# Counting edges in groups of 125 with 12 targets: one-hots on three engines and count products pinned inside the units of a GNN and mixture-of-experts kernel

## The chip, the core and the metric

The kernel runs on one core of one Trainium2 chip. Its time is the device time in microseconds (us) of one execution; three executions were timed. A further execution was profiled, and all rows below come from that one.

## The reference, cut to what matters

1250 tokens of 1024 features go through a two-layer graph network over 40000 edges and then through a mixture of eight experts. Only the graph part is touched.

```python
def _sage_layer(h, edge_src, edge_dst, deg_inv, W_self, W_neigh, b):
    msg = h[edge_src]
    agg = jax.ops.segment_sum(msg, edge_dst, num_segments=h.shape[0])
    mean = agg * deg_inv[:, None]
    return h @ W_self + mean @ W_neigh + b
deg = jax.ops.segment_sum(jnp.ones_like(edge_dst, dtype=x.dtype), edge_dst, num_segments=N)
deg_inv = 1.0 / jnp.maximum(deg, 1.0)
h = jax.nn.relu(_sage_layer(x, edge_src, edge_dst, deg_inv, W_self0, W_neigh0, b0))
out = _sage_layer(h, edge_src, edge_dst, deg_inv, W_self1, W_neigh1, b1)
```

The edges come sorted by target (`edge_dst`).

## The kernel before

**Counts in place of a gather.** The segment sum is made a matrix product: a matrix C counts how often source s sends to target t, kept as 10 blocks of 128 sources by 1250 targets. The neighbour sum of a layer is then a product of C with the features, and the column sums of C are the degrees. C must be complete before the first of these products, at line 553.

**How C is filled.** The sorted edges are cut into 160 groups of 250 (`EG`), each two chunks of 125 edges (`GC`, `GP`). All targets of a group lie within 24 (`WIN`) of its first. For a chunk, GpSimd writes a one-hot `ol` of the source's lane (125 edges by 128 lanes, line 413), VectorE a one-hot `oh` of the source's block and the target's place in the window (125 by 10 x 24 = 240, line 420), and TensorE multiplies them (line 423). The two chunks of a group add up in PSUM tile `cnt`; VectorE then adds the 128 x 240 counts into C at the group's base (line 442). The base is a number in `base_i`, which VectorE's sequencer loads into a register (line 437) before the add can be issued. `row_of_groups` does two groups, four chunks, at a time; there are 80 rows. The adds of a row are issued two rows later (`open_rows`). If a group did not fit its window, `verdict` would say so and a second, general path would run after the first.

**What stands around it.** `self_unit` computes a 128-column piece of h @ W_self for a range of tokens: eight matrix products over k, each of 256, 498 or 496 columns. There are 24 of them. `y_unit` computes h @ W_neigh for 128 tokens, ten in the first quarter (q == 0); its result is split into a high part by ScalarE and a low part by VectorE (`split`, line 394). The whole of the counting is spread over self units and the ten y units of q == 0. After them come the column sums (line 553) and the products with C (line 564).

**What sets the order.** The opening, up to the first `turn_ranges`, is in an order written out by hand for VectorE, ScalarE and TensorE (`manual_schedule`). Rows of groups are then asked for by `some_groups(n)` ahead of a unit, and the scheduler of the build places each instruction in its engine's queue; each engine then runs its queue strictly in that order. `keep_in_program_order` pins an instruction against earlier pinned ones. `routing_constants` (small VectorE work, and a transfer of `eb2` that VectorE reads) is pinned so, after the units of q == 1.

**Buffers.** `hot` has six buffers for each of `ol` and `oh`; `pc` has three PSUM banks for `cnt`, so a row of groups can start only when the adds of the row three before it are done.

Of the kernel before, what the change touches and what calls it, by code (L numbers as in the profile page):

```python
# [20 lines left out]

P = 128
EPS = 1e-5
WIN = 24
GC, GP = 2, 125
LQ = 32


# [1 line left out]
def kernel(  # L30
# [28 lines left out]
    QW = D // 4  # L59
    NB = -(-N // P)  # L60
    NP = NB * P
    EG = GC * GP
    NGR = NE // EG
    R = NGR // 2
    WEXP = KD * H + KH * D
    NTILE = (2 * N) // P + E
    assert R * 2 * EG == NE and R <= P and 2 * NB * WIN <= 512 and N > WIN
    rows = [min(P, N - b * P) for b in range(NB)]

    step = -(-(N - 2 * P) // 4) * 2  # L70
# [72 lines left out]
    stt = nc.vector.scalar_tensor_tensor  # L143


    RE = 2 * EG
    assert 8 * RE <= 4000 and 3 * NGR <= 500 and 8480 + 6 * NGR <= 9440
    edge = L[:R, 4000:8000].rearrange("p (a n) -> p a n", n=RE)
    dst_i, src_i, hi_i, lo_i = (edge[:, a, :].bitcast(I32) for a in range(4))
    dst_f, hi_f, lo_f, key = (edge[:, a, :] for a in range(4, 8))  # L150
# [13 lines left out]
    nc.vector.memset(eps, EPS)  # L164

    nc.scalar.activation(small.tile([P, 1], F32, name="rs"), eps, AF.Sqrt)
    ident = const.tile([P, P], F32, name="ident")
    make_identity(nc, ident)

# [27 lines left out]
    nc.scalar.dma_start(out=b0_p, in_=b0.rearrange("(k p) -> p k", p=P))  # L197


    ext = const.tile([R, 3, 2], F32, name="ext")  # L200
    base_i = const.tile([1, NGR], I32, name="base_i")

    keys = const.tile([GP, 2, 2 * GC, R], F32, name="keys")
    worst = const.tile([1, 1], F32, name="worst")
    plain = const.tile([1, 1], I32, name="plain")
    gx = L[:1, 8000 : 8000 + 3 * NGR].rearrange("o (a g) -> o a g", a=3)
    lo_, hi_ = gx[:, 0, :], gx[:, 1, :]
    APART = 16
    assert APART * EG < 4096

    dst_halves = dst_f.rearrange("p (a n) -> p a n", a=2)

    def make_keys():

        nc.vector.tensor_reduce(ext[:, 0, :], dst_halves, AX.X, ALU.min)
        nc.vector.tensor_scalar(ext[:, 2, :], ext[:, 0, :], float(N - WIN), None, op0=ALU.min)
        nc.vector.tensor_scalar(hi_i, src_i, 7, None, op0=ALU.arith_shift_right)
        nc.vector.tensor_scalar(lo_i, src_i, P - 1, None, op0=ALU.bitwise_and)
        nc.vector.tensor_copy(hi_f, hi_i)
        nc.vector.tensor_copy(lo_f, lo_i)  # L220
        stt(key, hi_f, float(WIN), dst_f, op0=ALU.mult, op1=ALU.add)
        for i in range(2):
            part = key[:, i * EG : (i + 1) * EG]
            nc.vector.tensor_scalar(part, part, ext[:, 2, i : i + 1], None, op0=ALU.subtract)

    def turn_keys():
        for a, v in enumerate((key, lo_f)):
            ps = tpp.tile([P, 4, P], F32, name="tp")
            pf = ps.rearrange("p a b -> p (a b)")
            for c in range(2 * GC):  # L230
                nc.tensor.transpose(
                    pf[:GP, c * R : (c + 1) * R], v[:, c * GP : (c + 1) * GP], ident[:R, :R]
                )
            nc.scalar.copy(keys[:, a].rearrange("p c g -> p (c g)"), pf[:GP, : 2 * GC * R])

    def turn_ranges():

        nc.vector.tensor_reduce(ext[:, 1, :], dst_halves, AX.X, ALU.max)
        for a in (2, 0, 1):
            pe = tpp.tile([P, 4, P], F32, name="tp")  # L240
            for i in range(2):
                nc.tensor.transpose(pe[:1, i, :R], ext[:, a, i : i + 1], ident[:R, :R])
            nc.vector.tensor_copy(
                gx[:, a, :].rearrange("o (r i) -> o i r", i=2), pe[:1, :2, :R]
            )
            if a == 2:
                nc.vector.tensor_copy(base_i, gx[:, 2, :])

    def verdict():

        bad = L[:1, 8480 : 8480 + 6 * NGR].rearrange("o (a g) -> o a g", a=6)
        nc.vector.memset(bad, -1.0)
        stt(bad[:, 0, :], hi_, float(1 - WIN), lo_, op0=ALU.add, op1=ALU.subtract)
        nc.vector.tensor_tensor(bad[:, 1, : NGR - 1], lo_[:, : NGR - 1], lo_[:, 1:], ALU.subtract)
        nc.vector.tensor_tensor(bad[:, 2, : NGR - 1], hi_[:, : NGR - 1], hi_[:, 1:], ALU.subtract)
        stt(
            bad[:, 3, : NGR - APART], hi_[:, : NGR - APART], 1.0, lo_[:, APART:],
            op0=ALU.add, op1=ALU.subtract,
        )
        nc.vector.tensor_scalar(bad[:, 4, :], hi_, float(1 - N), None, op0=ALU.add)  # L260
        nc.vector.tensor_scalar(bad[:, 5, :], lo_, -1.0, None, op0=ALU.mult)
        nc.vector.tensor_reduce(worst, bad.rearrange("o a g -> o (a g)"), AX.X, ALU.max)
        nc.vector.tensor_scalar(plain, worst, 0.0, None, op0=ALU.is_le)
# [93 lines left out]
    def gnn_windows():  # L357
# [22 lines left out]

        y0 = ExitStack()
        yp = y0.enter_context(tc.tile_pool(name="yp", bufs=1, side="right"))
        hot = y0.enter_context(tc.tile_pool(name="hot", bufs=6, side="right"))

        yh = yp.tile([P, NB, QW], F32R, name="yh")
        yl = yp.tile([P, NB, QW], F32R, name="yl")
        win = yp.tile([P, NB * WIN], F16, name="win")
        win_i = yp.tile([P, NB * WIN], I32, name="win_i")
        nc.gpsimd.iota(win_i, pattern=[[1, NB * WIN]], base=0, channel_multiplier=0)
# [18 lines left out]
        GW = NB * WIN  # L408

        def row_of_groups(r):  # L410
            ol = hot.tile([GP, 2 * GC, P], F16, name="ol")
            for c in range(2 * GC):
                nc.gpsimd.tensor_scalar(  # L413
                    ol[:, c, :], lane[:GP], keys[:, 1, c, r : r + 1], None, op0=ALU.is_equal
                )
            ps = pc.tile([P, 2, 256], F32, name="cnt")
            for i in range(2):
                for c in range(GC):
                    oh = hot.tile([GP, GW], F16, name="oh")
                    nc.vector.tensor_scalar(  # L420
                        oh, win[:GP], keys[:, 0, i * GC + c, r : r + 1], None, op0=ALU.is_equal
                    )
                    nc.tensor.matmul(  # L423
                        ps[:, i, :GW], ol[:, i * GC + c, :], oh,
                        start=(c == 0), stop=(c == GC - 1),
                    )
            open_rows.append((r, ps))
            if len(open_rows) > 2:
                close_row()

        open_rows = []

        def close_row():
            r, ps = open_rows.pop(0)
            for i in range(2):
                g = 2 * r + i
                at = nc.values_load(
                    base_i[0:1, g : g + 1], engines=(ENG.DVE,), min_val=0, max_val=N - WIN,
                    skip_runtime_bounds_check_because="cut at N - WIN, and a target is never below 0",
                )  # L440
                to = C[:, :, ds(at, WIN)]
                nc.vector.tensor_tensor(  # L442
                    to, to.bitcast(F32),
                    ps[:, i, :GW].rearrange("p (k w) -> p k w", k=NB), ALU.add,
                )

        groups = iter(range(R))

# [4 lines left out]
                    row_of_groups(g)  # L453


        def self_unit(w, d, c, halfway=None):
            c0, n = cchunks[c]
            ps = mm.tile([P, 512], F32, name="ps")
            for k in range(KD):
                if halfway is not None and k == KD // 2:  # L460
                    halfway()
                nc.tensor.matmul(  # L462
                    ps[:, :n], w[:, k, (d % 2) * P : (d % 2 + 1) * P], h0T[:, k, c0 : c0 + n],
                    start=(k == 0), stop=(k == KD - 1),
                )
            nc.scalar.activation(
                hT1[:, d, c0 : c0 + n], ps[:, :n], AF.Identity, bias=b0_p[:, d : d + 1]
            )


        with tc.manual_schedule(engines={ENG.DVE, ENG.Activation, ENG.PE}):
            norm = [layernorm_steps(first_row_of(b), first_row_of(b), P) for b in range(6)]

            def step(*bs):
                for b in bs:
                    next(norm[b])

            step(0, 0, 1, 0, 1)
            turn_tokens(0)
            nc.vector.tensor_copy(dst_f, dst_i)  # L480
# [17 lines left out]
            clear(9)  # L498
            turn_ranges()
        w_next = load_q(w_self0, 1)  # L500
        some_groups(3)
        tokens(6)
        tokens(7)
        some_groups(2)
        self_unit(ws_first, 1, 1)
        tokens(8)
        tokens(9)
        some_groups(2)
        self_unit(ws_first, 0, 2)
        some_groups(2)  # L510
        self_unit(ws_first, 1, 2)
        verdict()
        for q in range(1, 4):
            w_q = w_next
            w_next = load_q(w_self0, q + 1) if q < 3 else load_q(w_neigh0, 0)
            for d in (2 * q, 2 * q + 1):
                for c in range(3):
                    some_groups(4 if c else 2)
                    self_unit(w_q, d, c)
            if q == 1:  # L520
                routing_constants()

# [13 lines left out]
        for q in range(4):  # L536
            w_q = w_next
            w_next = load_q(w_neigh0, q + 1) if q < 3 else None
            for b in range(NB):
                if q == 0:  # L540
                    some_groups(1)
                y_unit(w_q, h0T, b, yh[: rows[b], b, :], yl[: rows[b], b, :])
            if q == 3:
                w_half = load_half(w_neigh1, 0)
            if q == 0:
                some_groups(R)
                while open_rows:
                    close_row()

                for c0, n in cchunks:  # L550
                    ps = mm.tile([P, 512], F32, name="ps")
# [1130 lines left out]
```

## Time and profile before

| | us |
|---|---|
| runs shown: median (lowest to highest) | 1147.37 (1146.6 to 1149.48) |
| the profiled execution, its own time | 1146.48 |
| its span, first to last instruction | 1144.3 |
| first one-hot `oh` starts | 31.6 |
| first count product starts | 35.1 |
| last count product starts | 232.8 |
| column sums of C (line 553) start | 234.6 |
| busy from 28.6 to 234.6: TensorE, VectorE, ScalarE, GpSimd | 201.7, 153.9, 25.3, 193.2 |

The span is cut into 40 slices of 28.6 us. The counting lies in slices 2 to 9. A busy time counts an instruction from its start to its modelled end, so that a queue of short instructions can look fuller than it is; where a pace matters, the distance from one start to the next is the better number. A matrix product in 32-bit floats stands in the trace as two records.

### The profile page before, as it was taken

What the parts mean: (1) busy time and instruction counts of PE and PEld (TensorE: products, weight loads), DVE (VectorE), ACT (ScalarE), POOL (GpSimd) and SP (SyncE); (2) the same over time, 40 slices, a digit from 0 to 9 for tenths busy, and PEclk for the clock granted to TensorE, in tenths of its full rate; (3) what the DMA queues carried; (4) which work ended last, traced back from release to release, by engine and by line L of the source; (5) the groups of instructions that cost most, each with busy time, mean ns of one, the idle gap of its engine ahead of it and who ended that gap; (6) DMA issues with size and microseconds to landing.
All of it is one profiled execution on the core that took longest, in us unless ns stands there. A gap on an engine that the chain in (4) does not pass through costs nothing.

```text
span 1144.3 us, 13214 instructions
## 1 busy us (share of the span) xinstructions
PE 1108.3 (97%) x4775; PEld 791.2 (69%) x4775; DVE 451.1 (39%) x1129; ACT 181.5 (16%) x420; POOL 331.7 (29%) x438
## 2 busy tenths in 40 slices
PE   6999999999999999999999999999999989999994
PEld 4556556888888886887688778885444766666662
DVE  8777777761212154341224132555322542111110
ACT  5301000001111111100110000123011223222220
POOL 1899999800000000032003002342000013223221
PEclk9999999999999999999999999999999999999997
DMA  6110111010100021042004261335921435444542
GB/s 230 34 38 5 38 38 38 1 37 1 38 1 1 1 74 38 1 154 93 7 10 168 88 222 42 117 148 209 373 60 37 150 92 136 112 113 105 127 115 45
DMA packets 59330, 95.40 MB, mean 83 GB/s; under 512 B 8797, under 2 KB 35645, under 8 KB 59251
## 3 DMA queue, kind: packets, MB, share of 16 engines
q1 hardware_dynamic: 48400, 67.72, 17.3%
q0 software_dynamic: 7056, 23.88, 9.2%
q10 hardware_dynamic: 3798, 2.84, 0.8%
q8 instruction: 42, 0.69, 0.2%
q14 instruction: 34, 0.28, 0.1%
HBM read 68.76 MB, written 27.47 MB: 84 GB/s over the span
## 4 chain that ended last, share of the span: by engine, by line
PE 93%; DVE 2%; ACT 1%; DMA 1%; POOL 1%; issue 0%; ACTq 0%; DVEq 0%; POOLq 0%
PE ps L528 12%; PE ps L462 11%; PE psb L642 9%; PE ps L712 8%; PE ps L564 8%; PE ps L642 7%; PE ps L1516 7%; PE ps L1541 7%; PE ps L1188 5%; PE ps L629 5%; PE ps L1202 4%; PE cnt L423 3%; PE tp L1504 2%; PE ps L1141 2%; PE ps L1537 1%; PE tp L322 1%
## 5 line engine op out<-in xcount | busy, mean ns | idle before, releaser
L413 POOL TENSOR_SCALAR ol<-lane,keys 125x128 f16<-125x128 f16 x320 | 193.2, 622 | 27.6 <-DVE oh L420 27.6
L462 PE MATMUL ps<-h0T,L 128*128 128x498 f32 (+2 forms) x384 | 147.4, 518 | 0.2 <-ACT h0T L325 0.2
L528 PE MATMUL ps<-L,h0T 128*128 128x256 f32 (+1 forms) x640 | 142.0, 380 | 0.0
L708 POOL TENSOR_TENSOR L<-L 128x512 f32<-128x512 f32 (+1 forms) x20 | 31.4, 1576 | 375.1 <-DMA L<-in_L_gnn_b_dram 216.5
L528 PEld LDWEIGHTS ps<-L,h0T 128*128 128x128 f32 (+1 forms) x640 | 118.7, 188 | 17.7 <-issue 0.5
L420 DVE TENSOR_SCALAR oh<-win,keys 125x240 f16<-125x240 f16 x320 | 84.7, 322 | 32.7 <-PE cnt L423 31.1
L462 PEld LDWEIGHTS ps<-h0T,L 128*128 128x128 f32 x384 | 68.1, 192 | 38.3 <-issue 33.9
L1516 PE MATMUL ps<-xw,L 128*128 x368 | 84.9, 384 | 0.4 <-issue 0.4
L1541 PE MATMUL ps<-xw,L 128*128 x184 | 83.5, 597 | 0.1
L564 PE MATMUL ps<-C,yh 128*128 128x256 f32 (+2 forms) x240 | 81.9, 356 | 0.0
L564 PE MATMUL ps<-C,yl 128*128 128x256 f32 (+2 forms) x240 | 81.5, 354 | 0.0
L712 PE MATMUL ps<-zh,C 128*128 128x512 f32 (+1 forms) x200 | 79.6, 398 | 0.0
L712 PE MATMUL ps<-zl,C 128*128 128x512 f32 (+1 forms) x200 | 78.7, 393 | 0.0
L1516 PEld LDWEIGHTS ps<-xw,L 128*128 128x128 f32 x368 | 69.2, 193 | 10.3 <-issue 1.8
L1552 POOL DMA_INDIRECT out_dram<-L x23 | 36.3, 1579 | 133.5 <-ACT L L1505 87.9
L442 DVE TENSOR_TENSOR C<-C,cnt 128x240 f32 x160 | 64.3, 402 | 12.5 <-DVE oh L420 1.6
L1493 POOL DMA_INDIRECT L<-t_d,L x26 | 26.0, 1000 | 148.1 <-DVE L L141 127.8
L1541 PEld LDWEIGHTS ps<-xw,L 128*128 128x128 f32 x184 | 33.3, 190 | 35.3 <-issue 32.9
L423 PEld LDWEIGHTS <-ol 125*128 125x128 f16 x320 | 30.9, 97 | 36.7 <-POOL ol L413 20.0
L1549 DVE TENSOR_SCALAR L<-ps,L 128x512 f32<-128x512 f32 x23 | 17.3, 751 | 91.8 <-PE ps L1541 91.8
L394 DVE TENSOR_TENSOR yl<-ps,yh 128x256 fp32r<-128x256 f32 (+1 forms) x40 | 16.9, 424 | 92.1 <-ACT yh L393 92.1
L423 PE MATMUL cnt<-oh,ol 125*128 125x240 f16 x320 | 50.0, 266 | 2.6 <-POOL ol L413 2.1
(226 smaller groups left out, 1504.3 us busy)
## 6 DMA issues: line engine op xcount, KB each, us to landing
xw<-in_L_ffn_ew_dram SPq DMA_DIRECT2D x16, 1024.0 KB, 7.6
L<-in_x_dram SPq DMA_DIRECT2D x20, 256.0 KB, 2.8
v_d<-L SPq DMA_DIRECT2D x18, 256.0 KB, 2.0
xa<-v_d SPq DMA_DIRECT2D x18, 256.0 KB, 6.0
t_d<-L SPq DMA_DIRECT2D x9, 512.0 KB, 4.0
out_dram<-xa SPq DMA_DIRECT2D x9, 512.0 KB, 3.7
L<-in_L_gnn_W_self_dram SPq DMA_DIRECT2D x4, 1024.0 KB, 5.4
L<-in_L_gnn_W_neigh_dram SPq DMA_DIRECT2D x4, 1024.0 KB
```

Source lines behind the costliest of these rows:

```text
L413: nc.gpsimd.tensor_scalar(ol[:, c, :], lane[:GP], keys[:, 1, c, r : r + 1], None, op0=ALU.is_equal)
L420: nc.vector.tensor_scalar(oh, win[:GP], keys[:, 0, i * GC + c, r : r + 1], None, op0=ALU.is_equal)
L423: nc.tensor.matmul(ps[:, i, :GW], ol[:, i * GC + c, :], oh, start=(c == 0), stop=(c == GC - 1),)
L442: nc.vector.tensor_tensor(to, to.bitcast(F32), ps[:, i, :GW].rearrange("p (k w) -> p k w", k=NB), ALU.add,)
L462: nc.tensor.matmul(ps[:, :n], w[:, k, (d % 2) * P : (d % 2 + 1) * P], h0T[:, k, c0 : c0 + n], start=(k == 0), stop=(k == KD - 1),)
L528: nc.tensor.matmul(ps[:m, :QW], hT[:, k, blk(b)], w[:, k, :], start=(k == 0), stop=(k == KD - 1))
L564: nc.tensor.matmul(ps[:, :n], part[: rows[k], k, (d % 2) * P : (d % 2 + 1) * P], C[: rows[k], k, c0 : c0 + n], start=(k == 0 and part is y ...
L629: nc.tensor.matmul(ps[:m], hT1[:, k, blk(b)], w[:, k, :], start=(k == 0), stop=(k == KD - 1))
L642: nc.tensor.matmul(ps, rows_of(k), w[:, k, :], start=(first and k == 0), stop=(k == KB - 1), skip_group_check=not first,)
L712: nc.tensor.matmul(ps[:m], C[: rows[k], k, blk(b)], part[: rows[k], k, :], start=(k == 0 and part is yh), stop=(k == NB - 1 and part is yl),)
L1516: nc.tensor.matmul(ps[:, :H], xT[:, k, :], w1_all[:, ds(e, 1), k * H : (k + 1) * H], start=(k == 0), stop=(k == KD - 1),)
L1541: nc.tensor.matmul(ps, hT[:, q, :], w2_all[:, ds(e, 1), q * D + h * HALF : q * D + (h + 1) * HALF], start=False, stop=(q == KH - 1),)
```

## The change

- **Smaller groups.** A group is now one chunk of 125 edges with a window of 12 targets: `EG` = 125, `WIN` = 12, and `RG` = 4 groups in a row. There are still 80 rows and 320 count products, each of 120 columns in place of 240. Each product is a group of its own, so there are 320 adds of 128 x 120 in place of 160 of 128 x 240, each with its own register load.
- **One-hots spread.** Of a row's four `ol`, GpSimd makes two and ScalarE two, each by two activations, relu(1 - |key - lane|). Of its four `oh`, VectorE makes three and GpSimd the fourth.
- **Rings.** `oh` has 14 buffers, `ol` and the new `away` four.
- **Order.** VectorE's one-hots, the adds, the count products and the products of `self_unit` are pinned. `self_unit` takes a number of rows and spreads them over its eight products; the three units of a 128-column piece get 2, 4 and 3 rows. One add follows each product, eight groups behind. `y_unit` is not pinned. The last eight adds come after the last y unit in the program.
- **Opening.** Sixteen products of the identity with itself stand ahead of the first transposes.
- **Smaller things.** `base_i` has 320 numbers, and the rows of `verdict` are twice as long; `ext`, `base_i` and `keys` move to another pool; `bad` lies over the edge lists.

```diff
-WIN = 24
-GC, GP = 2, 125
+WIN = 12
+EG = 125
+RG = 4
...
-        hot = y0.enter_context(tc.tile_pool(name="hot", bufs=6, side="right"))
+        hot = y0.enter_context(tc.tile_pool(name="hot", bufs=4, side="right"))
+        hot_t = y0.enter_context(tc.tile_pool(name="hot_t", bufs=14, side="right"))
...
         def row_of_groups(r):
-            ol = hot.tile([GP, 2 * GC, P], F16, name="ol")
-            for c in range(2 * GC):
-                nc.gpsimd.tensor_scalar(
-                    ol[:, c, :], lane[:GP], keys[:, 1, c, r : r + 1], None, op0=ALU.is_equal
-                )
-            ps = pc.tile([P, 2, 256], F32, name="cnt")
-            for i in range(2):
-                for c in range(GC):
-                    oh = hot.tile([GP, GW], F16, name="oh")
-                    nc.vector.tensor_scalar(
-                        oh, win[:GP], keys[:, 0, i * GC + c, r : r + 1], None, op0=ALU.is_equal
-                    )
-                    nc.tensor.matmul(
-                        ps[:, i, :GW], ol[:, i * GC + c, :], oh,
-                        start=(c == 0), stop=(c == GC - 1),
-                    )
-            open_rows.append((r, ps))
-            if len(open_rows) > 2:
-                close_row()
...
+            ol = hot.tile([EG, RG, P], F16, name="ol")
+            for i in range(RG):
+                k = keys[:, 1, i, r : r + 1]
+                if i < 2:
+                    nc.gpsimd.tensor_scalar(ol[:, i, :], lane[:EG], k, None, op0=ALU.is_equal)
+                else:
+
+                    away = hot.tile([EG, P], F16, name="away")
+                    nc.scalar.activation(away, lane[:EG], AF.Abs, scale=-1.0, bias=k)
+                    nc.scalar.activation(ol[:, i, :], away, AF.Relu, scale=-1.0, bias=one_p[:EG])
+            ps = pc.tile([P, RG, P], F32, name="cnt")
+            for i in range(RG):
+                oh = hot_t.tile([EG, GW], F16, name="oh")
+                eng = nc.vector if i < RG - 1 else nc.gpsimd
+                made = eng.tensor_scalar(
+                    oh, win[:EG], keys[:, 0, i, r : r + 1], None, op0=ALU.is_equal
+                )
+                if i < RG - 1:
+                    pin(made)
+                pin(nc.tensor.matmul(ps[:, i, :GW], ol[:, i, :], oh, start=True, stop=True))
+
+                if len(to_add) >= 2 * RG:
+                    add_group()
+            to_add.extend((r, ps, i) for i in range(RG))
+
+        to_add = []
+        pin = tc.keep_in_program_order
+
+        def add_group():
+            r, ps, i = to_add.pop(0)
+            g = RG * r + i
+            at = nc.values_load(
+                base_i[0:1, g : g + 1], engines=(ENG.DVE,), min_val=0, max_val=N - WIN,
...
+            )
+            to = C[:, :, ds(at, WIN)]
+            tc.keep_in_program_order(
                 nc.vector.tensor_tensor(
                     to, to.bitcast(F32),
                     ps[:, i, :GW].rearrange("p (k w) -> p k w", k=NB), ALU.add,
                 )
+            )
...
-        def self_unit(w, d, c, halfway=None):
+        def self_unit(w, d, c, halfway=None, n_groups=0):
...
-                nc.tensor.matmul(
-                    ps[:, :n], w[:, k, (d % 2) * P : (d % 2 + 1) * P], h0T[:, k, c0 : c0 + n],
-                    start=(k == 0), stop=(k == KD - 1),
+                some_groups(((k + 1) * n_groups) // KD - (k * n_groups) // KD)
+                pin(
+                    nc.tensor.matmul(
+                        ps[:, :n], w[:, k, (d % 2) * P : (d % 2 + 1) * P], h0T[:, k, c0 : c0 + n],
+                        start=(k == 0), stop=(k == KD - 1),
+                    )
                 )
...
+            idle = mm.tile([P, 512], F32, name="ps")
+            for _ in range(16):
+                nc.tensor.matmul(idle[:, :P], ident, ident, start=True, stop=True)
             step(0, 0, 1, 0, 1)
...
         w_next = load_q(w_self0, 1)
-        some_groups(3)
-        tokens(6)
-        tokens(7)
-        some_groups(2)
-        self_unit(ws_first, 1, 1)
-        tokens(8)
-        tokens(9)
-        some_groups(2)
-        self_unit(ws_first, 0, 2)
-        some_groups(2)
-        self_unit(ws_first, 1, 2)
+        self_unit(ws_first, 1, 1, None, 3)
+        for b in range(6, NB):
+            tokens(b)
+            some_groups(1)
+        self_unit(ws_first, 0, 2, None, 3)
+        self_unit(ws_first, 1, 2, None, 3)
         verdict()
...
                 for c in range(3):
-                    some_groups(4 if c else 2)
-                    self_unit(w_q, d, c)
+                    self_unit(w_q, d, c, None, (2, 4, 3)[c])
...
                 if q == 0:
-                    some_groups(1)
+                    some_groups(2 if b < 4 else b < NB - 1)
                 y_unit(w_q, h0T, b, yh[: rows[b], b, :], yl[: rows[b], b, :])
...
                 some_groups(R)
-                while open_rows:
-                    close_row()
+                while to_add:
+                    add_group()
```

## The prediction

> **What bounds the kernel now.** I read the busy row and the slices first, then the chain of waits, then the groups, and last the records of single lines.
>
> ```profile
> PE 1108.3 (97%) x4775; PEld 791.2 (69%) x4775; DVE 451.1 (39%) x1129; ACT 181.5 (16%) x420; POOL 331.7 (29%) x438
> ...
> PE   6999999999999999999999999999999989999994
> PEld 4556556888888886887688778885444766666662
> DVE  8777777761212154341224132555322542111110
> ACT  5301000001111111100110000123011223222220
> POOL 1899999800000000032003002342000013223221
> ```
>
> TensorE (PE) is full from slice 2 on. But its weight loads (PEld) are thin in slices 2 to 8, and exactly there GpSimd (POOL) is full: the counting stage. All other stages are left as they are, so the change is worth what it does to the start of the column sums of C at 234.62 us; what follows is TensorE work in an unbroken chain, and moves with it.
>
> ```profile
> 229.16 3.47 PE ps L528 x16
> 234.62 6.00 PE ps L553 x30
> ```
>
> In the list of the chain the start comes first, then the length: the last-but-one y unit, and the column sums.
>
> ```profile
> L413 POOL TENSOR_SCALAR ol<-lane,keys 125x128 f16<-125x128 f16 x320 | 193.2, 622 | 27.6 <-DVE oh L420 27.6
> L420 DVE TENSOR_SCALAR oh<-win,keys 125x240 f16<-125x240 f16 x320 | 84.7, 322 | 32.7 <-PE cnt L423 31.1
> L442 DVE TENSOR_TENSOR C<-C,cnt 128x240 f32 x160 | 64.3, 402 | 12.5 <-DVE oh L420 1.6
> L423 PE MATMUL cnt<-oh,ol 125*128 125x240 f16 x320 | 50.0, 266 | 2.6 <-POOL ol L413 2.1
> ```
>
> GpSimd's 193.2 us run from 32.1 to 225 without a gap: 2.42 us a row of groups. Yet TensorE lost little by it: from one product's start to the next is 102 ns at the median, and over the 229 neighbouring pairs the excess is 28.5 - 229 x 0.102 = 5.1 us. Of the 198 us from the first product to the last, the products are 320 x 0.102 = 32.6.
>
> The number that decides is in the records of VectorE's sequencer (DVEq), which count as idle in the busy rows:
>
> ```profile
> L437 DVEq TENSOR_LOAD <-base_i x160: 297/303/551, 37.6 to 233.7; - x160
> ...
> L442 DVEq FUSED_REGOPS x160: 69/69/69, 38.3 to 234.0; - x160
> ```
>
> (least/median/most ns.) Each add needs a register load of 303 ns, a gap of 76, and register arithmetic of 69 before it is issued, and the next load starts only after that. From load to load with only an add between, 73 pairs in the trace have a median of 531 ns (least 513), although the add itself keeps the engine about 0.4 us. Today that is 160 x 0.53 = 85 us of 200, and hidden.
>
> **The change, part by part.**
>
> *Narrower products.* 120 columns in place of 240. The 240-column pitch of 102 ns is 2.4 columns a ns, so 120 columns are 51 ns, if the weight load keeps up. The Trainium skill, "TensorE: Matmul & The Clock Gate", section "Back-to-back issue gap", speaks against that: it gives a load-and-multiply pair about 81 ns at 128 columns. The rows that are near: at line 1359 pairs with 16-bit weights of 128x128 follow one another every 25 ns with 23 columns and 34 ns with 69. So the load isn't the floor here and I take 51: 320 x 0.051 = 16.3 us saved; by the page's figure 6.7.
>
> *GpSimd.* Two `ol` of 604 ns (193.2/320) and one `oh` of at most that: 1.8 us a row. TensorE asks for a row every 2.07 us in the units: a piece has 3.46 + 6.67 + 6.64 us of own products (pitches of 216 and 416 ns a record) and nine rows of 4 x 0.051 = 0.2. So GpSimd is no bound any more, and the 5.1 us of stalls go. ScalarE gets four activations a row; from its 128x256 cast (372 ns) and 128x1 activation (about 300) a 128-column one is about 0.33, so 1.3 a row beside 0.68 for every third: it fits, and the order waits of its queue cost nothing while rings are four rows deep.
>
> *What is late next: VectorE's sequencer.* Adds double to 320. Per row: four times 0.531 for load and add, three one-hots between loads at 0.035 (pairs with one one-hot between have 562 ns at least), and, as compiled, one add in four waits on two semaphores, which puts an extra event of 21 ns ahead (two such adds in the trace were 68 ns later). Sum 2.12 + 0.10 + 0.07 = **2.30 us a row**, against 2.07 that TensorE would take. The data path isn't the limit: 120 columns of add and one-hot are shorter than that. The Trainium skill, "DMA: Bandwidth & Descriptors", section "Latency and other measured facts", puts a register load's floor at about 600 ns; with 0.3 more per load a row would be 3.5 us, and 80 rows end 90 us later. The trace has 303 for this very load, so that is out.
>
> Now the pinned order: a product needs its one-hot, and the one-hots stand between the adds. TensorE can therefore not run ahead of VectorE by more than the one-hots allow, and waits.
>
> - 54 rows lie in the 18 units of q 1 to 3: 54 x (2.30 - 2.07) = 12.4 us.
> - `verdict` took 55.02 to 57.6 = 2.6 us of VectorE; rows twice as long add 0.17 (160 elements at 0.96 a ns, the slope between the 960-element reduction of 1.14 us and the 160-element ones) to four operations, 0.1 to two, 1.0 to the reduction: 4.5, of which a load behind it hides 0.5. It had slack before; now 4.0 are seen.
> - `routing_constants`: 1.6 us of small operations and 1.2 of casts; and the first cast waits for the `eb2` transfer, which landed 3.95 us after the last memset that SP's queue waits for. As compiled five adds (2.7) stand between, so 1.3 is waited for. Together 4.1; 4.5 with the row's late one-hots.
> - The third group of `turn_ranges` now waits for a copy with no product to fill in: 0.5.
>
> *The tail.* As compiled, the low-part split of the tenth y unit stands ahead of the last **eleven** adds in VectorE's queue. Today two adds stand there, and the column sums start 1.86 us after the last product:
>
> ```profile
> 233.05 0.42 DVE L394 TENSOR_TENSOR yl<-ps,yh 98x256 fp32r<-98x256 f32 x1 [1.32 <-ACT yh L393]
> 233.64 0.93 DVE L442 TENSOR_TENSOR C<-C,cnt 128x240 f32 x2 [0.16 <-DVE yl L394]
> ```
>
> After: the unit's drain 0.17 (its products are 380 ns long and 216 apart), ScalarE's half 0.37 (its cast at line 393), issue 0.1, 11 x 0.531 + 3 x 0.07 = 6.05, the last add 0.3: 7.0 us from the last y product.
>
> *Warm-up.* The identity is ready at 1.45 us, 16 products at the slow pitch of 213 ns end at 4.9, and the first transpose waits for VectorE until 9.10. TensorE's first 16 transposes ran at 213 ns each, later ones at 109; the speed changed near 15.2 (the granted clock in the windows says 1.00 throughout and doesn't show it). The same page on TensorE, section "What's actually happening", has the clock throttled again after an idle window of some 3.4 us; the gap is 4.2. So I take nothing; the other end is 1.6 us earlier keys, of which VectorE, busy until 34.4 with its norms and a longer memset, passes on 0.7.
>
> *The rest.* The test for the window is met: in the drawn edges the widest group of 125 spans a distance of 9 targets, and 11 fit. Pools and the longer `base_i` copies lie beside waiting engines: nothing, 0.3 if not.
>
> **The sum.** Last product today 232.8; less 16.3, less 5.1: 211.4. Plus 12.4, 4.0, 4.5 and 0.5: 232.8. The last y product ends 0.2 before; plus 7.0: column sums at 239.6, that is 5.0 later than 234.6. Small waits that I can't sum (the fourth one-hot late behind two `ol`, 0.1 to 0.9 here and there) only add: I take 5.8. The profiled execution of 1146.5 becomes 1152.3; the median lay 0.9 above it, so **1153** for the runs.
>
> **Rivals.**
>
> 1. *TensorE stays the bound; VectorE keeps up.* Then 16.3 + 5.1 go, and the tail gives back about 5: 1131. It needs a load-and-add of at most (2.07 - 0.17)/4 = 0.47 us. Against it: not one of the 73 pairs is under 0.513. For it: the pairs never had a row's pattern in a long stretch. 7%.
> 2. *About even.* VectorE at its least values (0.513: 5.8 less over 80 rows), `verdict` and the constants partly covered by the two rows by which VectorE may run ahead: 1145 to 1150.5. 18%.
> 3. *Worse than my sum.* A pair costs 0.54 and a one-hot 0.05, as in crowded stretches (pairs of 535 to 539 are common): 2.4 us a row, 0.1 x 67 = 7 more; or the product is held at 81 ns, and 2 to 3 more where VectorE isn't the bound: 1158 to 1164. 20%.
> 4. *The test fails and the second path runs*: excluded by the edges' own numbers, save for a mistake of mine; it would double the time. Below 1%.
>
> My own case has 55%, from 1150.8 to 1157. A measurement of this kernel tells a change from none at about 0.3%, 3.4 us: from my case nearly all is slower, case 2 is same to two thirds. So slower 0.76, same 0.16, faster 0.08. The range of 8 in 10 leaves out case 1 and the ends: 1147.5 to 1161.
>
> **What would show it.** Right: register loads about 0.56 us apart through most of 40 to 200; VectorE's one-hot the releaser of the count products in place of GpSimd's `ol`; gaps of 3 to 6 us on TensorE at `verdict` and the constants; GpSimd with pauses; products 51 ns apart where nothing waits; eleven adds between the last split and line 567's start. Wrong: TensorE without gaps in slices 2 to 7 (rival 1), or loads closer than 0.5 us; if the waits are on GpSimd's `oh` or ScalarE's `ol`, the spread itself is the bound.

## The result, and the profile after

The changed kernel takes **1163.74 us** (median of four runs, 1163.28 to 1164.6), the kernel before 1146.98 on the same chip (four runs, 1146.28 to 1149.48): a ratio of **1.0146, 95% interval 1.0134 to 1.0158**. It is slower, as forecast, but by 16.8 us where 6 were forecast, and outside the range. The profiled execution took 1163.42, its span 1161.6. First the busy row and slices of the changed kernel (29 us each):

```profile
PE 1110.1 (96%) x4813; PEld 790.5 (68%) x4813; DVE 449.7 (39%) x1212; ACT 280.7 (24%) x740; POOL 280.9 (24%) x358
...
PE   7898899979999999999999999999999989999993
PEld 6444555768888886888688768885444666666661
DVE  7876777553121236233134132454422532111110
ACT  5865565501111111110010000023111223232220
POOL 1776676500000000004003101343000013223221
PEclk9999899989999999999999999999999999999997
```

TensorE now has holes in slices 2 to 9. GpSimd, once full there, is at five to seven tenths up to slice 8, VectorE at five to eight: by slices no engine is full where time is lost. PEclk, the granted clock, has dips in slices 5 and 9, where the kernel before has none. The chain of waits (start, length) shows how much the counting takes:

```profile
241.73 0.91 PE ps L542 x4
...
249.28 7.63 PE ps L567 x30
256.91 5.25 PE ps L578 x42
```

The column sums start at 249.28 instead of 234.62, 14.7 later (forecast: 5.0, with small waits 5.8), and take 7.63 instead of 6.00. All after that adds 1.0. The groups of the whole run (busy, mean ns, then the idle time just before and who ended it), and the records of VectorE's sequencer:

```profile
L420 POOL TENSOR_SCALAR ol<-lane,keys 125x128 f16<-125x128 f16 x160 | 97.0, 617 | 87.5 <-PE cnt L435 56.2 <-ACT keys L233 28.8 <-ACT away L424 2.0
L453 DVE TENSOR_TENSOR C<-C,cnt 128x120 f32 x320 | 89.3, 279 | 55.4 <-DVE C L453 17.2 <-PE cnt L435 16.1 <-DVE oh L430 3.5
L430 POOL TENSOR_SCALAR oh<-win,keys 125x120 f16<-125x120 f16 x80 | 46.8, 587 | 0.7 <-PE cnt L435 0.7
L435 PE MATMUL cnt<-oh,ol 125*128 125x120 f16 x320 | 36.1, 217 | 15.1 <-DVE oh L430 7.0 <-POOL oh L430 5.1 <-DVE C L453 0.8
```

```profile
L447 DVEq TENSOR_LOAD <-base_i x320: 296/301/547, 37.6 to 248.5; - x160
...
L453 DVEq FUSED_REGOPS  x320: 69/69/69, 38.3 to 248.8; - x160
```

The loads are what the forecast took them for, and VectorE's one-hot is the first releaser of the products. But GpSimd's `ol` waited 56.2 us *for products*, and products in turn waited 5.1 us for GpSimd's `oh`. A bound engine doesn't wait; an engine with slack isn't waited for. Both at once point to a closed round.

### The profile page after: what moved, and what is told of

Its sections match the earlier page's. It is cut to its first block, busy times and chain, and to the rows that moved or that the text cites. A ratio compares the mean times of both kernels' runs of the same rounds, so it can differ in the third digit from the quotient of the medians.

```text
span 1161.6 us, 14004 instructions
## 1 busy us (share of the span) xinstructions
PE 1110.1 (96%) x4813; PEld 790.5 (68%) x4813; DVE 449.7 (39%) x1212; ACT 280.7 (24%) x740; POOL 280.9 (24%) x358
## 4 chain that ended last, share of the span: by engine, by line
PE 84%; DVE 5%; POOL 3%; DMA 2%; issue 2%; DVEq 1%; ACT 1%; POOLq 0%; ACTq 0%; SPq 0%
PE ps L542 12%; PE psb L656 9%; PE ps L726 8%; PE ps L578 8%; PE ps L656 7%; PE ps L1530 7%; PE ps L1555 7%; PE ps L1202 5%; PE ps L643 5%; PE ps L477 4%; PE ps L1216 4%; DVE C L453 3%; PE ps L1155 2%; POOL ol L420 2%; PE tp L1518 2%
## 5 line engine op out<-in xcount | busy, mean ns | idle before, releaser
L477 PE MATMUL ps<-h0T,L 128*128 128x498 f32 (+2 forms) x384 | 151.4, 529 | 1.5 <-ACT rs L335 1.0
L542 PEld LDWEIGHTS ps<-L,h0T 128*128 128x128 f32 (+1 forms) x640 | 119.0, 187 | 21.1 <-DVE C L453 2.0
L420 POOL TENSOR_SCALAR ol<-lane,keys 125x128 f16<-125x128 f16 x160 | 97.0, 617 | 87.5 <-PE cnt L435 56.2
L453 DVE TENSOR_TENSOR C<-C,cnt 128x120 f32 x320 | 89.3, 279 | 55.4 <-DVE C L453 17.2
L425 ACT ACTIVATE ol<-away,one_p 125x128 f16<-125x128 f16 x160 | 56.0, 396 | 72.8 <-PE cnt L435 72.8
L430 DVE TENSOR_SCALAR oh<-win,keys 125x120 f16<-125x120 f16 x240 | 63.5, 270 | 0.0
L424 ACT ACTIVATE away<-lane,keys 125x128 f16<-125x128 f16 x160 | 56.1, 390 | 0.0
L399 DVE TENSOR_TENSOR yl<-ps,yh 128x256 fp32r<-128x256 f32 (+1 forms) x40 | 16.9, 423 | 94.4 <-ACT yh L398 94.4
```

Of the source, the lines that this page charges most:

```text
L420: nc.gpsimd.tensor_scalar(ol[:, i, :], lane[:EG], k, None, op0=ALU.is_equal)
L430: made = eng.tensor_scalar(oh, win[:EG], keys[:, 0, i, r : r + 1], None, op0=ALU.is_equal)
L453: nc.vector.tensor_tensor(to, to.bitcast(F32), ps[:, i, :GW].rearrange("p (k w) -> p k w", k=NB), ALU.add,)
L477: nc.tensor.matmul(ps[:, :n], w[:, k, (d % 2) * P : (d % 2 + 1) * P], h0T[:, k, c0 : c0 + n], start=(k == 0), stop=(k == KD - 1),)
L542: nc.tensor.matmul(ps[:m, :QW], hT[:, k, blk(b)], w[:, k, :], start=(k == 0), stop=(k == KD - 1))
```

## Where the time went

For each stage I take TensorE's time from the start of one unit to the start of the next, less its own work (pitches of 216 and 417 ns a record, 102 or 52 a product), in both traces. The difference, after less before:

| stage | us |
|---|---|
| opening, to the first own-part unit of 498 columns | +1.1 |
| from there to the end of the last token block (28 products) | +1.1 |
| rest of the first part, `verdict`, second part | +4.8 |
| `routing_constants` | +8.1 |
| third and fourth part | +7.5 |
| y units | +2.7 |
| behind the last y product | +4.8 |
| narrower products | -16.0 |

The sum is 14.1; the start times say 14.7. Of the difference, 0.4 is work of TensorE that the change adds: `turn_ranges` has twelve small transposes instead of six, 0.07 us apart. The forecast had pacing and `verdict` at 16.4 (15.0 in the table), the tail at 5.0 and the constants at 4.5; and it took 5.1 off for stalls, which the first two rows don't show at all. In the third and fourth part most of the loss lies in the 498-column units, which carry four rows: 1.6 to 1.75 us each, 0.06 in the kernel before.

## The experiments

Each kernel was timed beside the kernel before. In short (the changed kernel: 1.0146):

| kernel | median us | ratio to before, interval |
|---|---|---|
| e1 one register load a row | 1160.40 | 1.0117, 1.0100 to 1.0134 |
| e2 constants spread | 1156.94 | 1.0085, 1.0068 to 1.0102 |
| e3 last rows earlier | 1157.33 | 1.0100, 1.0083 to 1.0117 |
| e4 fourth one-hot on VectorE, 13 rows | 1164.84 | 1.0152, 1.0135 to 1.0169 |
| e5 GpSimd in program order | 1158.31 | 1.0084, 1.0064 to 1.0104 |
| e6 = e1 + e5 | 1140.33 | 0.9928, 0.9911 to 0.9946 |
| e7 = e1, ring of eight | 1165.24 | 1.0147, 1.0130 to 1.0165 |
| e8 = e1 + e5 + e2 + e3 | 1131.62 | 0.9853, 0.9834 to 0.9873 |
| e9 no warm-up | 1163.48 | 1.0127, 1.0107 to 1.0146 |
| e10 clock kept | 1164.93 | 1.0147, 1.0127 to 1.0167 |
| e11 before, with e1's and e2's edits | 1157.67 | 1.0083, 1.0066 to 1.0099 |
| e12 no `verdict` | 1160.34 | 1.0107, 1.0091 to 1.0123 |

The kernel before took 1146.9 us beside e1 to e4, 1148.5 beside e5 to e8 and 1147.5 beside e9 to e12, so across these groups the ratios are the safer comparison.

### Is it VectorE's sequencer? (e1)

```diff
-            at = nc.values_load(base_i[0:1, g : g + 1], ...)
-            to = C[:, :, ds(at, WIN)]
+            if i == 0:
+                _, starts[:] = nc.values_load_multi_w_load_instructions(
+                    base_i[0:1, RG * r : RG * r + RG], ...)
+            to = C[:, :, ds(starts[i], WIN)]
```

> One register load brings the four window bases of a row of groups, in place of one load before each add; products, one-hots, pins and everything else stay. Theory A (VectorE's sequencer sets the pace of the rows): a row loses three loads of 0.30 us, so it takes about 1.4 us of VectorE instead of 2.2 to 2.3, less than TensorE's 2.07; the 15 us of pacing in the own-part and y units go, and of the 11 adds behind the tenth split (7.0 us) eight loads of 0.3, 2.4 us: 1163.7 falls by 14 to 18 us, to 1146 to 1150. Theory B (the one-hots that GpSimd and ScalarE now make, or the pinned order, set the pace, and VectorE only waits with them): at most 3 us go, 1160 to 1164.

Only 3.3 us went: theory A, the forecast's own, is not enough. TensorE loses 2.2 us at the constants instead of 8.1 and waits 1.6 less in the tail, but in between it loses more than in the changed kernel. From the second unit of one 128-column piece to that of the next (nine rows of groups), TensorE takes in the three such stretches after the constants:

| kernel | us |
|---|---|
| before | 20.6, 20.4, 20.4 |
| changed | 20.2, 21.2, 21.0 |
| e1 | 21.3, 21.4, 21.4 |
| e5 | 19.2, 19.2, 19.2 |
| e6 | 19.2, 19.2, 19.2 |

In e1 VectorE's three loads a row are gone and the pace has not moved. These are e1's groups for about that stretch (119.7 to 204):

```profile
L420 POOL TENSOR_SCALAR ol<-lane,keys 125x128 f16<-125x128 f16 x72 | 44.7, 633 | 21.1 <-PE cnt L435 21.1
L454 DVE TENSOR_TENSOR C<-C,cnt 128x120 f32 x141 | 38.2, 271 | 29.6 <-PE cnt L435 28.0 <-DVE C L454 1.5
...
L430 POOL TENSOR_SCALAR oh<-win,keys 125x120 f16<-125x120 f16 x35 | 20.2, 576 | 0.0
```

The add (line 454 here) waits 28.0 us for products: VectorE is no longer the bound, and something else has the same pace. The lane one-hot waits 21.1 for products, and GpSimd's `oh` behind it for nothing. The timeline of the changed kernel shows why; first GpSimd, then TensorE (start, length, instruction, count, and idle before it):

```profile
147.13 0.64 POOL L430 TENSOR_SCALAR oh<-win,keys 125x120 f16<-125x120 f16 x1
148.20 1.21 POOL L420 TENSOR_SCALAR ol<-lane,keys 125x128 f16<-125x128 f16 x2 [0.43 <-PE cnt L435]
149.39 0.58 POOL L430 TENSOR_SCALAR oh<-win,keys 125x120 f16<-125x120 f16 x1
```

```profile
147.34 0.32 PE L435 MATMUL cnt<-oh,ol 125*128 125x120 f16 x3
147.82 0.21 PE L435 MATMUL cnt<-oh,ol 125*128 125x120 f16 x1 [0.16 <-POOL oh L430]
...
149.59 0.64 PE L435 MATMUL cnt<-oh,ol 125*128 125x120 f16 x4
```

Counted through the records, the `oh` at 147.13 is that of row 43, the product at 147.82 its fourth, the two `ol` at 148.20 those of row **47**, and the `oh` at 149.39 that of row 44. VectorE's one-hots, the adds and the products are pinned; GpSimd is not, and the scheduler put each row's `oh` behind the `ol` of the row three further on. The ring of `ol` has four buffers, so the `ol` of row 47 needs the last product of row 43, that product needs the `oh` of row 43, and the `oh` of row 44 stands behind both `ol`. The round is 0.64, 0.05 to the product, 0.21, 0.17 to the `ol`, and 1.19 to the next `oh`: 2.26 us from `oh` to `oh`, of which GpSimd works only some 1.8. Most rounds in the units with four rows take 2.17 to 2.26. (The three products in 0.32 us are 52 ns apart, the last one taking 0.21.)

### Which of the two chains? (e5, e6, e7)

e5 pins GpSimd too; e6 is e5 with e1's load; e7 is e1 with `hot` at eight buffers, unpinned.

```diff
-                    nc.gpsimd.tensor_scalar(ol[:, i, :], ...)
+                    pin(nc.gpsimd.tensor_scalar(ol[:, i, :], ...))
...
-                if i < RG - 1:
-                    pin(made)
+                pin(made)
```

> GpSimd's instructions are pinned to the order of the program too: the two lane one-hots of a row, then its fourth target one-hot, row by row; in the changed kernel a row's fourth target one-hot stands behind the lane one-hots of the row three further on, which wait for the product of the row before. Each base is loaded on its own as in the changed kernel. Theory C (two chains of about 2.2 us a row lie beside each other: VectorE's sequencer, and a closed round of GpSimd one-hot 0.58, product 0.21, two lane one-hots 1.25 and three hand-overs): VectorE still sets the pace, so at most 4 us go, 1160 to 1164, some of it in the stage beside the last token blocks. Theory D (GpSimd's round alone sets the pace): 12 to 16 us go, 1148 to 1152.

> GpSimd in the order of the program, and one register load for the four bases of a row: both suspected chains are shortened (VectorE to about 1.4 us a row, GpSimd to the 1.8 us that its three one-hots take). Theory C: TensorE's own 2.07 us a row is left as the bound, the 15 us of pacing go, and 2 to 3 of the tail: 1145 to 1149, where either alone leaves 1160 or more. If a third thing sets the pace (ScalarE's four passes, the ring of counts in PSUM): above 1156.

> One load for the four bases as in the first experiment, and the ring of lane one-hots eight deep instead of four, GpSimd's order left to the scheduler. The scheduler then puts a row's fourth target one-hot behind the lane one-hots of the row seven further on, so the round GpSimd one-hot, product, lane one-hots is closed as before. Theory C: within 2 us of the first experiment's 1160.4. If it was the depth of the ring and not the place in GpSimd's queue: 1146 to 1150, as with the order pinned.

One load alone brings 0.29% (e1), the order alone 0.62% (e5), **both 2.18%**, more than twice the sum. That is the mark of two limits beside each other (theory C): taking one away shows the other. In the traces of e5 and e6 each row's `oh` does follow that row's `ol`, in all 80 rows. e5's groups from 125.1 to 203, and the busy times of e6 from 110 to 186 (columns: length, then PE, PEld, DVE, ACT, POOL busy and counts, granted clock, DMA):

```profile
L420 POOL TENSOR_SCALAR ol<-lane,keys 125x128 f16<-125x128 f16 x70 | 41.7, 608 | 0.0
L452 DVE TENSOR_TENSOR C<-C,cnt 128x120 f32 x136 | 38.1, 280 | 20.5 <-DVE C L452 8.5 <-DVE oh L430 1.9 <-PE cnt L434 1.6
```

```profile
110.00:186.00 76.00, 76.00 (x331) 42.07 (x330) 48.59 (x248) 48.11 (x152) 62.72 (x107) 1.00 0.07 23
```

In e5 the lane one-hots wait for nothing, and the add waits for VectorE's own adds instead of products. Its rows of loads still come every 2.26 us, one in eight or nine after 2.6: 2.30 on average. In the third and fourth part TensorE nevertheless runs at its own 19.2, since VectorE lives on what the rings hold; it has no slack, so `verdict` and the constants cost all the more (4.1 and 9.3 us by the measure of the table above). The total lies 1.7 us below what theory C allowed (3.4 by the ratio) and far from theory D's: the order alone sets the pace where VectorE has rings to live on, and VectorE sets it elsewhere. In e6 TensorE is busy 76.00 of 76.00 us, and the time is 5 us better than theory C's, because VectorE's slack now also covers most of `verdict` and the constants (2.0 us are lost at the constants instead of 8.1).

e7 comes out slower than e1, by 4.8 us or by 3.4 as the ratios have it, where 2 were allowed, and nowhere near 1150: a deeper ring alone opens nothing. GpSimd then works seven rows of `ol` ahead of each `oh`, the round is closed as before (2.25 us between neighbouring rows in the middle units, e1 2.245), and the long run-up costs 6 us more than in e1 before the last token block is done.

### Constants, tail and verdict (e2, e3, e12)

e2 issues the constants' transfers at the start of the second part and places the VectorE work in four lots:

```diff
+        constants = routing_constants()
         for q in range(1, 4):
...
-            if q == 1:
-                routing_constants()
+                    if c == 1:
+                        next(constants, None)
```

> The routing constants are no block behind the second part any more: their loads are issued at the start of that part, and their 20 VectorE instructions stand in four small lots behind the middle pieces of parts two and three. Theory A (the block holds up every one-hot behind it, TensorE is idle for 5.9 us and then runs 6.8 us at half clock): 6 to 8 us go, 1155.5 to 1158. Theory B (only the 1.7 us wait for the last of the loads is real; the instructions themselves cost their time wherever they stand, since VectorE is the bound): about 2 us go, 1161.5 to 1162.

Theory A held: 6.8 us. The busy times of the changed kernel from the constants on, and of e2 for the same place:

```profile
112.80:118.75 5.95, 0.39 (x2) 0.00 (x1) 2.80 (x14) 0.10 (x1) 0.67 (x2) 0.81 0.33 19
118.75:123.20 4.45, 4.45 (x17) 3.47 (x17) 3.59 (x18) 1.29 (x4) 1.85 (x3) 0.50 0.70 216
```

```profile
112.00:118.00 6.00, 5.85 (x32) 4.30 (x31) 4.35 (x19) 3.68 (x11) 4.48 (x8) 1.00 0.51 174
```

In the changed kernel TensorE works 0.39 of 5.95 us, and then 4.45 us at a clock of **0.50**. VectorE itself is busy only 2.80 of these. The wait for `eb2` is 1.7 of the rest, and nearly all the other 1.4 lie before adds whose bases are being loaded:

```profile
116.14 0.22 DVE L300 CAST L<-L 64x128 bf16<-64x128 f32 x1 [1.66 <-DMA L<-in_L_ffn_eb_dram]
```

e3 asks for the last rows earlier and makes the open adds before the ninth y unit:

```diff
-                    some_groups(2 if b < 4 else b < NB - 1)
+                    some_groups(2 if b < 6 else b == 6)
+                    if b > 6:
+                        for _ in range(4):
+                            if to_add:
+                                add_group()
```

> The last 13 rows stand two ahead of each of the first six y products and one ahead of the seventh, and the eight adds that are then still open are made ahead of the eighth and ninth y product, so that none stands behind the tenth split. Theory A (the 11 adds behind the last split are a tail of 7.0 us, 5.8 of them TensorE idle, and bring 1.6 us of half clock to the column sums): 5 to 7.5 us go, 1156 to 1158.5. Theory B (VectorE is the bound all through the y units, so rows moved forward stall TensorE there instead): within 1.5 us of 1163.7.

6.4 us, theory A again. e3's chain has no adds between the last y unit and the column sums, which run at full clock:

```profile
240.54 4.38 PE ps L542 x20
244.92 5.71 PE ps L571 x30
```

e12 leaves the test of the windows out (`plain` is set to 1):

> The check that every group of edges fits its window (eight VectorE instructions on one partition) is left out and its result set to true. Theory A/C (VectorE has no slack at its place, so its 4 us are exposed): 3 to 4.5 us go, 1159 to 1161. If GpSimd's round leaves VectorE slack there: under 1.5 us, 1162.3 to 1163.7.

3.4 us, within A/C. But they do not go where `verdict` stands: there e12's profile gains 0.3. VectorE comes to the constants less late, TensorE loses 3.9 there instead of 8.1, and the clock is halved for 3.4 instead of 6.8 us. VectorE's lateness is carried along and paid at the next place without a reserve.

### The clock and the warm-up (e9, e10)

> The 16 products of the identity with itself at the start are left out (they feed nothing). In the changed kernel they bring full clock at 7.2 us, but the first piece's eviction waits for the bias load until 18.6 all the same, TensorE stands still 2.8 us before 24.7 and runs 3.4 us at half clock. Theory E (the lead is spent in that wait, and the later half-clock stretch is its price): the third piece starts at 27.1 again as in the kernel before, 1 us earlier: 1162 to 1163.5. If the warm-up is worth something: 1164.5 to 1166.

> 54 products of yh with itself, 256 columns, about 0.11 us each and used by nothing, stand behind the last y product, so that TensorE is busy for 5.9 of the 6.65 us in which it waits for the last adds to C. Theory F (a stretch without work of TensorE is what halves its clock afterwards): the column sums run at full clock and take 6.0 us instead of 7.6, 1161.5 to 1162.5. If the clock falls for another reason, 7.6 us again and 1163.5 to 1164.5.

e10 puts 54 unused products behind the last y unit. The changed kernel's column sums, then e10's stretch with these products and its column sums:

```profile
249.28:256.70 7.42, 7.42 (x30) 6.57 (x31) 4.16 (x4) 0.00 (x0) 0.00 (x0) 0.75 0.00 0
```

```profile
245.90:253.19 7.29, 6.84 (x59) 6.80 (x59) 3.50 (x12) 0.37 (x1) 0.00 (x0) 1.00 0.45 144
253.19:258.90 5.71, 5.71 (x32) 4.97 (x31) 4.19 (x4) 0.00 (x0) 0.00 (x0) 1.00 0.00 0
```

5.71 us at a clock of 1.00 instead of 7.42 at 0.75: where TensorE is kept busy, the clock stays, which is theory F's mechanism. Its total (1161.5 to 1162.5) is missed: the run takes 1164.93, so no gain is shown. The column sums start 0.65 later after the last y product, since 14 of the 54 stand ahead of the last four count products, and this execution had other half-clock stretches early on. e9's third piece starts at 27.15 as theory E has it (28.23 in the changed kernel, 27.14 before), but its total can't be told from the changed kernel's: it was at half clock from 51.0 to 57.8, where the changed kernel's profile was not. The first is e9, the second the changed kernel:

```profile
50.90:57.80 6.90, 5.69 (x11) 2.51 (x11) 4.56 (x21) 4.25 (x14) 3.75 (x8) 0.51 0.00 1
```

```profile
50.90:57.80 6.90, 5.37 (x26) 2.77 (x25) 4.60 (x21) 5.34 (x18) 5.42 (x9) 1.00 0.01 4
```

Whether a wait of TensorE in this stage brings a half-clock stretch changes from trace to trace (the last section shows on what it turns) and costs some 2 us (e1, at half clock from 53.9 to 57.3, loses 1.8 more than the changed kernel there); differences of that size between single profiles are not read here.

### Two misses (e4, e11)

> In the first 13 rows (those beside the last token blocks and the first part) the fourth target one-hot of a row is made by VectorE instead of GpSimd; the other 67 rows stay. Theory A (in this stage TensorE waits for the fourth one-hot, which GpSimd makes last of its three): 3 to 5 us go, 1158.5 to 1161. Theory B (VectorE is the bound there too, with the normalisations of the last four blocks): 13 times 0.28 us are added, up to 1167.

No gain (1.0152): neither theory's number. Up to the end of the last token block (28 products) TensorE lost as much as in the changed kernel, 5.3 us. The products' waits for one-hots there, 1.5 us for VectorE's and 1.1 for GpSimd's, are gone; in their place TensorE waits 3.0 us for ScalarE's copies of the token blocks into `h0T`. These stand in ScalarE's queue behind its own activations for `ol`, and ScalarE has no pause from 45.4 to 54.7. The end of it, first ScalarE, then TensorE:

```profile
50.95 0.99 ACT L424 ACTIVATE away<-lane,keys 125x128 f16<-125x128 f16 x3
51.84 0.68 ACT L425 ACTIVATE ol<-away,one_p 125x128 f16<-125x128 f16 x2
52.42 0.68 ACT L424 ACTIVATE away<-lane,keys 125x128 f16<-125x128 f16 x2
53.01 0.85 ACT L324 COPY h0T<-tp 128x392 f32<-128x392 f32 x2
```

```profile
53.53 1.52 PE L477 MATMUL ps<-h0T,L 128*128 128x496 f32 x3 [1.66 <-ACT h0T L324]
```

So ScalarE is a third limit in this stage. No run here moves the copies ahead or takes `ol` off ScalarE, so what it is worth stays open. With both chains shortened (e6) the stage still loses 2.9, and 4.2 in the kernel before.

> The kernel before the change, with one register load for the two bases of a row and with the routing constants in small lots; its GpSimd makes nothing but lane one-hots, so there is no order to pin. Theory C (before, TensorE was the bound from the middle of the own part on, and neither VectorE's loads nor the constants cost it anything): 1145 to 1148, no difference, so that what the all-four version gains over it is the 16 us of narrower products. If these edits help any kernel alike: 1130 to 1140.

It is 10 us slower than the kernel before, which no theory had. In it the scheduler, which is free to place the products there, set them earlier: 280 stand before the end of the first y unit instead of 264, while GpSimd, with four `ol` a row, was busy 71.0 of 71.0 us from 124 to 195 and couldn't follow; TensorE was busy 67.1 of these. One load for two bases also takes 0.53 us there, hardly less than the two of 0.30 that it replaces. Which of the two edits upset the order was not tried.

### All together (e8)

> GpSimd's order, one load a row, the routing constants in small lots and the last rows earlier, together. From the sum: 1163.7 less 15 to 17 for the pace, less 6.8 for the constants, less 4 to 6 for the tail: 1135 to 1140, below the 1147 of the kernel before. If VectorE was what made the constants and the tail dear, these two are worth less beside the one load: up to 1144.

**1131.62 us, 1.5% faster than the kernel before**, and 3 us better than the sum's better end. The counting's end in e8's chain:

```profile
211.15 8.69 PE ps L546 x40
219.84 5.72 PE ps L575 x30
```

The column sums follow the y units without a gap, some 15 us before those of the kernel before.

## Why the prediction was right and wrong

- **Narrower products, 16.3 us:** right. They are 52 ns apart, not the 81 of the Trainium skill ("TensorE: Matmul & The Clock Gate", section "Back-to-back issue gap") that it was weighed against: 320 times 50 ns less, 16.0 us. That e8 is 16.9 faster than the kernel before agrees, but other terms go into that: it gains 1.9 behind the last y product and loses 1.5 in the third and fourth part.
- **"So GpSimd is no bound any more, and the 5.1 us of stalls go": this is the step that failed.** The 1.8 us a row were right, but they were weighed against TensorE's 2.07 as a sum of work. What counts is the order in GpSimd's queue, and there the three one-hots, a product and their hand-overs form a round of 2.2. Taking it away (e5) brings 5.4 us by the medians, 7.1 by the ratios, of the 10.7 by which the forecast was short, and leaves VectorE as the bound, which is the case that the forecast described. The credit of 5.1 was too large besides: even in e6 the stage where most of the stalls lay gets back only 1.3. There ScalarE's passes, which the forecast let fit at 0.33 us each and put at nothing, take 0.39 and hold up the copies (e4).
- **VectorE's sequencer, 2.30 us a row:** right in size (2.26 to 2.30), and incomplete as a cause. GpSimd's round has nearly the same pace, so removing the loads alone (e1) shows almost nothing; the two hid each other. TensorE's own row is 2.13 (19.2 / 9), not 2.07: beside the products the change of kind costs some 0.06. Pacing and `verdict` came to 15.0 where 16.4 were summed.
- **`verdict`, 4.0:** 3.4 (e12), but paid at the constants.
- **`routing_constants`, 4.5:** 8.1, and e2 takes 6.8 off the time. The wait was 5.9 long, and the half clock after it, 2.2 us, was not in the sum.
- **Tail:** from the last y product to the column sums, with the eleven adds in between, it took 7.03 us (242.25 to 249.28), forecast 7.0. Not in the sum: the column sums at half clock, 1.6.
- **Warm-up, nothing:** right in time (e9), wrong in its working. A 32-bit product is two records of 213 ns, so the 16 take 6.55 us, not 3.4, and the gap to the first transpose is 0.9, not 4.2. The first is the changed kernel, the second the one before:

```profile
1.50 6.55 PE L497 MATMUL ps<-ident 128*128 128x128 f32 x32 [1.50 <-POOL ident masks.py:199]
8.96 1.09 PE L321 MATMUL tp<-ident,L 128*128 128x128 f32 x8 [0.90 <-DVE L L338]
```

```profile
9.10 1.94 PE L322 MATMUL tp<-ident,L 128*128 128x128 f32 x8 [9.10 <-DVE L L339]
```

The first transposes do run at twice the speed. The lead of 1 us ends in the wait of the first unit's eviction for the bias (18.71), after which TensorE stands still before 24.64 and starts again at half clock:

```profile
18.71 0.48 ACT L482 ACTIVATE L<-ps,b_p 128x256 f32<-128x256 f32 x1 [1.03 <-DMA b_p<-in_L_gnn_b_dram]
...
24.64 3.48 PE L321 MATMUL tp<-ident,L 128*128 128x128 f32 x16 [2.51 <-ACT h0T L324]
```

- **Rivals.** The time fell into the third one's range, but not by its mechanisms: loads were not dearer and the products not held at 81 ns. The first (TensorE stays the bound, 1131) is what e8 measures, once both chains, the block of constants and the tail are gone. The forecast named "waits on GpSimd's `oh`" as the sign that the spread itself is the bound; that sign is there.

## What to carry to other kernels

An engine's work per row tells whether it *can* keep up; whether it does is decided by the order of its queue. Where some engines of a producer and consumer loop are pinned and one is left to the scheduler, look for an instruction that stands behind another that waits, through a ring, for what the first one releases; a deeper ring moved this round and didn't open it (e7). And where taking away the chain that surely limits brings nothing, look for a second one of the same pace before the theory is dropped: only both edits together show what either is worth.

## What was not expected of the hardware

- **What halves the clock is a window, not the length of a wait.** Between the opening and the column sums, TensorE's granted clock was 0.50 in stretches of 3.41, 6.83 and, once, 10.24 us. In each trace they begin whole multiples of 3.413 us apart; in the changed kernel (at 24.29, 116.44 and 246.15) it is 27 and 38 of them. Cut along this grid from 20 to 262 us, the 14 traces have 925 windows that are not at half clock already. In 33 of them TensorE was busy for 0.49 of the time or less, and each was followed by half clock; in the other 892 it was busy for 0.499 or more, and none was. A window at half clock was followed by another if it was busy for up to 0.80, by full clock from 0.83 on. So a wait of 2.5 us at 22.1 in the changed kernel, all in one window, brings a stretch, and one of 2.2 us at 68.8 in e5, shared by two, does not. PE's busy time is the second number after the stretch:

```profile
20.88:24.29 3.41, 1.25 (x10) 0.94 (x8) 2.74 (x7) 3.41 (x6) 0.00 (x0) 1.00 0.25 68
```

```profile
66.96:70.37 3.41, 1.86 (x8) 1.13 (x6) 3.38 (x9) 2.81 (x9) 1.95 (x4) 1.00 0.50 133
70.37:73.79 3.42, 2.67 (x18) 2.14 (x19) 2.36 (x11) 0.20 (x1) 1.98 (x4) 1.00 0.68 175
```

  The grid lies elsewhere in each trace. That fits e9's stretch at 51 us: the window ahead of it was busy for 0.46, while the changed kernel's two windows from 48.2 to 55.0 have 0.57 and 0.55. Later in the traces, from 930 to 956, four windows busy for 0.55 to 0.63 were followed by half clock as well, so the limit is not as sharp everywhere.
- **A wait can cost more than its length:** 2.2 us on top of 5.9 at the constants, 1.6 on top of 6.65 at the column sums.
- **One register load brings four values in 0.34 us, but two take 0.53** (medians of e1 and e11), and one takes 0.30. Four loads a row are 1.2 us of VectorE's sequencer, one of four values is 0.34. Why two take longer than four is not known.
- **16-bit weight loads of 125 x 128 hide behind products of 120 columns**: 52 ns from start to start.
